# A second level of seven products for gate and up tiles 8 and 9 in a float32 recurrent block

## The chip, the cores and the metric

The kernel runs on one core of a Trainium2 chip. The metric is the time of one execution on the device in microseconds (us). The kernel before takes 2179.63 us as the median of three runs (2178.49 to 2179.87). The engines are named as the profile names them: PE is the matrix engine (PEld its weight loads), DVE the vector engine, ACT the scalar engine, POOL the GpSimd engine, and SP the engine that issues most DMAs.

## The reference, cut to what matters

x has shape 8 x 1024 x 512, all values are float32. One part of the block is a recurrent attention (`s`), the other a gated network (`g`) whose three weight matrices are looked up from 16 values:

```python
xn = layernorm(x)
gate = xn @ lut[gate_idx].T        # 1376 x 512 indices
up = xn @ lut[up_idx].T            # 1376 x 512 indices
h = silu(gate) * up
g = silu(h @ lut[down_idx].T)
out = x + s * g                    # s: three decayed causal scores over xn, gated, times Wo
```

The change touches only gate and up: for each of 8 batches, 1024 tokens by 1376 outputs, twice.

## The kernel before, in words

**Phase 1** (the first 606 us) normalizes and transposes x, runs the attention chunk by chunk, and in between builds the weight matrices from their indices: `ffn_weights` is a generator of which a few steps are taken after each piece of attention (`build_some`), and what is left is run off after the last chunk. Most of these steps are one or two DVE instructions; sums of weights are on POOL. The results go to DRAM.

**Phase 2** goes through the 8 batches: first gate and up, then the down projection (`down_pair`, four pairs of token chunks), which also adds x and writes the output.

Gate and up together are treated as one 2 x 2 block product and computed with seven products in place of eight (the scheme of Strassen and Winograd): the rows are gate and up of one output tile of 128, the columns are the halves of 512 tokens, and the contraction is two halves of 256. The 1376 outputs make eleven tiles: ten of 128 and a last of 96.

- Tiles 0 to 7 form two groups of four (`quads`, NQ = 2). There each of the seven products is itself computed with seven products of half its width, so one `Node` (line 713) stands for one outer product: 7 inner products, each for two pairs of tiles (`a` in 0, 1, side by side in one PSUM bank), each a float32 matmul of 256 columns. The profile counts two PE instructions for one float32 matmul, so that a node is 28 instructions at line 730. The inner products of the next node are mixed between those of the present one (`first`, `fifth` at lines 827 to 835), so that PE always has a product to do while DVE and ACT work on the banks. The output of a node goes through four steps `empty(t, n)`, one for each bank, which differ by outer product (lines 809 to 815).
- Tiles 8, 9 and 10 are done by `single` (line 671) with the outer seven products alone: 14 matmuls of 512 columns, 28 instructions at line 684. In batch 0, tiles 8 and 9 come before the groups of four, since the sums of x needed by the groups are not yet there; in batches 1 to 7 they come after them.

Four big temporaries hold partial results: `p1` and `u2` in pool `tmp`, `u3` and `e5` in pool `tmp2`. The singles take turns in `p1` and `u2`; `down_pair` uses all four. The weights of a node or a single come by a DMA on SP into `ring`, which has three buffers. The second level overwrites one block of x (`xs[:, :, 1, :]`) by a difference; the singles need the block itself, so it is loaded again at the end of the groups (`restore`, line 776, DMAs issued by POOL). `keep_order` at the end fixes the order of PE, DVE, ACT and POOL to the order of the program; SP's order is the planner's.

In phase 1, `gate_up(o)` (line 232) writes the weights of tile o for the singles to `wgu_d[o]`, and for every second tile below 8 also the weights of the second level to `quad_d` (lines 258 to 273): four POOL instructions over 128 x 896, three DMAs and six more steps of the generator.

Of the kernel before, what the change touches and what calls it, by code (L numbers as in the profile page):

```python
# [9 lines left out]
F32 = mybir.dt.float32  # L10
# [27 lines left out]
def recurrent_block(ctx: ExitStack, tc, x, wq, wk, wv, wo, wg, decay_logits, out_scale, lut, gidx, uidx, didx, out):  # L38
# [15 lines left out]

    nc = tc.nc
    B, T, V = x.shape
    D = wq.shape[1]
# [17 lines left out]

    wgu_d = [dram.tile([P, 14, m], F32, name=f"wgud{o}", tag=f"wgud{o}") for o, (_, m) in enumerate(OCH)]

    quad_d = [dram.tile([P, 7, 2, 7 * P], F32, name=f"quadd{q}", tag=f"quadd{q}") for q in range(NQ)]  # L80
    wd_d = [dram.tile([P, 7 * V // 2], F32, name=f"wdd{j}", tag=f"wdd{j}") for j in range(NK)]
    wdt_d = dram.tile([OCH[-1][1], V], F32, name="wdtd", tag="wdtd")
    xs_d = [dram.tile([P, 14, U], F32, name=f"xsd{b}", tag=f"xsd{b}") for b in range(B)]
# [139 lines left out]
    def ffn_weights(build, pool, pair_pool):  # L223
# [8 lines left out]
        def gate_up(o):  # L232
            s, m = OCH[o]
            n = 2 * NV * m
            idx = build.tile([P, NB], I32, name="idx", tag="idx", bufs=2)
            iv = idx[:, :n].rearrange("p (a b) -> p a b", b=m)
            gs, us = (src[:, s : s + m].rearrange("(c p) b -> p c b", p=P) for src in (gidx, uidx))
            nc.sync.dma_start(out=iv[:, 2:6, :], in_=gs)
            nc.sync.dma_start(out=iv[:, 0:2, :], in_=us[:, 0:2, :])
            nc.sync.dma_start(out=iv[:, 6:8, :], in_=us[:, 2:4, :])  # L240
            yield
            wf = pool.tile([P, 2 * NB], F32, name="wgu", tag="wgu", bufs=2)
            yield from look_up(build, wf[:, :n], idx[:, :n], P, n)
            w = wf[:, : 2 * n].rearrange("p (k two m) -> p k two m", two=2, m=m)
            a21, a11, a12, a22, s1, s2, s3, s4 = (w[:, k] for k in range(8))
            nc.gpsimd.tensor_tensor(s1, a21, a22, ALU.add)
            nc.gpsimd.tensor_tensor(s2, s1, a11, ALU.subtract)
            yield
            nc.gpsimd.tensor_tensor(s3, a11, a21, ALU.subtract)
            nc.gpsimd.tensor_tensor(s4, a12, s2, ALU.subtract)  # L250
            wide = wf[:, 2 * m : 2 * n].rearrange("p (a b) -> p a b", b=m)
            defer(3, lambda: nc.sync.dma_start(out=wgu_d[o], in_=wide))
            if o >= 4 * NQ:
                return
            if o % 2 == 0:
# [377 lines left out]
    def phase_2():  # L633
        with (
# [11 lines left out]
            def bank(role, name):  # L646
                return psp.tile([P, U], F32, name=name, tag=role)
# [20 lines left out]
                    nc.gpsimd.tensor_tensor(o, x1, x2, ALU.subtract)  # L668
                    yield

            def single(b, o, xs, h, h_tail, at_last):

                s, m = OCH[o]
                w = ring.tile([P, 14, P], F32, name=f"wr{b}_{o}", tag="wr")
# [1 line left out]
                ho = h[:, o, :] if o < 2 * NK else h_tail  # L676
                ha, hb = ho[:m, :U], ho[:m, U:]
                pa, pb, pe, pc = (bank(r, f"f{r}{b}_{o}")[:m, :] for r in ("s11", "s12", "sE", "s21"))
                t = tmp.tile([P, 4, U], F32, name=f"t{b}_{o}", tag=("u2", "p1")[o % 2])
                u2, u3, e, sg = (t[:m, k, :] for k in range(4))  # L680

                def product(ps, k, start, stop):
# [30 lines left out]
            class Node:  # L713
# [2 lines left out]

                def __init__(self, b, q, k, xs):
                    self.k, self.xs = k, xs  # L720
                    self.w = ring.tile([P, 2, 7, P], F32, name=f"wq{b}_{q}_{k}", tag="wr")
                    nc.sync.dma_start(
                        out=self.w.rearrange("p a t m -> p a (t m)"), in_=quad_d[q][:, W_OF[k], :, :]
                    )
                    self.t = [bank(r, f"{r}{b}_{q}_{k}") for r in ("s11", "s12", "s21", "sE")]
                    self.name = f"e{b}_{q}_{k}"

                def product(self, n, i, start=False):
                    for a in range(2):
                        nc.tensor.matmul(  # L730
                            self.t[n][:, ts(a, H)],
                            lhsT=self.w[:, a, (0, 1, 6, 2, 3, 4, 5)[i - 1], :],
                            rhs=self.xs[:, X_OF[self.k], D_OF[i], :],
                            start=start and a == 0,
                            stop=False,
                            skip_group_check=True,
                        )
# [17 lines left out]
                def seventh(self):  # L755
                    self.product(2, 7)
                    nc.vector.tensor_tensor(self.t[3], self.t[2], self.e, ALU.add)  # L757

            def quads(b, xs, h):


                def two(ap):
                    return ap.rearrange("p (a t) -> p a t", a=2)

                def steps(q):
                    p1, u2, u3, e5 = (
                        pool.tile([P, 4, U], F32, name=f"{k}{b}_{q}", tag=k)
                        for k, pool in (("p1", tmp), ("u2", tmp), ("u3", tmp2), ("e5", tmp2))
                    )

                    def of_h(half, n):
                        r, c = divmod(n, 2)
                        t = half * U + c * H
                        return h[:, 4 * q + r : 4 * q + r + 3 : 2, t : t + H]

                    def restore(*ks):

                        for k in ks if q == NQ - 1 else ():
                            nc.gpsimd.dma_start(out=xs[:, X_OF[k], 1, :], in_=xs_d[b][:, 2 * X_OF[k], H:])

                    def add(o, other):
                        return lambda t, n: nc.vector.tensor_tensor(o[:, n], t[n], other[:, n], ALU.add)  # L782
# [16 lines left out]

                    def after_7():  # L800
                        on_gpsimd(u2, e5)
                        restore(1, 6, 5, 7)

                    def after_4():
                        restore(2, 3, 4)
                        multiply(1, e5)
                        multiply(0, u3)

                    yield 1, lambda t, n: nc.scalar.copy(p1[:, n], t[n]), None
                    yield 6, add(u2, p1), None  # L810
                    yield 5, lambda t, n: nc.scalar.copy(e5[:, n], t[n]), None
                    yield 7, add(u3, u2), after_7
                    yield 2, add(p1, p1), lambda: on_gpsimd(e5, u3)
                    yield 3, node_3, None
                    yield 4, node_4, after_4

                todo = [(q, step) for q in range(NQ) for step in steps(q)]
                node = Node(b, 0, todo[0][1][0], xs)
                node.first()
                node.fifth()  # L820
                node.fifth_copy()
                for n, (q, (k, empty, after)) in enumerate(todo):
                    following = Node(b, todo[n + 1][0], todo[n + 1][1][0], xs) if n + 1 < len(todo) else None
                    node.sixth()
                    node.product(0, 2)
                    empty(node.t, 0)
                    if following:
                        following.first()
                    node.seventh()
                    empty(node.t, 3)  # L830
                    node.product(1, 3)
                    empty(node.t, 1)
                    if following:
                        following.fifth()
                        following.fifth_copy()
                    node.product(2, 4)
                    empty(node.t, 2)
                    if after:
                        after()
                    node = following  # L840

            def some(weights, n):
                for _ in range(n):
# [88 lines left out]
            for b in range(B):  # L932
# [11 lines left out]
                first_sums = sums_of_x(xs, True) if b == 0 else iter(())  # L944
                some(first_sums, 3)
                for o in early:
                    single(b, o, xs, h, h_tail, at_last)
                some(first_sums, 7)
                if b == 0:
                    nc.sync.dma_start(out=wd_tail[: OCH[-1][1], :], in_=wdt_d)  # L950
                    for src, dst in zip(wd_d, wd_sb):
                        nc.sync.dma_start(out=dst, in_=src)
                quads(b, xs, h)
                for o in range(4 * NQ, NO):
                    if o not in early:
                        single(b, o, xs, h, h_tail, at_last)
                t = got[-1]
                more = iter(())
                for c in range(NC // 2):
# [53 lines left out]
```

## Time and profile before

| What | Value |
|---|---|
| median of the runs | 2179.63 us |
| the profiled execution, its own time | 2179.92 us |
| its span, first to last instruction | 2178.1 us |
| granted PE clock | 1.000 |
| DVE, ACT, POOL busy | 51%, 38%, 42% |
| start of phase 2 on PE (line 684, batch 0) | 610.0 us |
| instructions at line 684 (singles), line 730 (nodes) | 672, 3136 |
| DMA, mean | 140 GB/s |

A row of the profile's groups reads: line, engine, operation, output <- inputs, shape, count, then busy time and the mean duration of one, then the idle time of the engine just before. PE's instructions overlap, so that the mean duration of one (380 ns for 256 columns) is longer than the distance to the next; a stretch of PE is therefore measured from start to start. A wait stands under the line that waited, with the engine and line that it waited for.

### The profile page before, as it was taken

The page shows a single profiled execution, that of the slowest core. Times are in us where ns is not written, and L with a number is a line of the kernel's source. Part 1 is how long each engine was busy: PE and PEld are TensorE (multiplying, and loading weights), DVE is VectorE, ACT ScalarE, POOL GpSimd, SP SyncE. Part 2 cuts the span into 40 slices and gives each one's busy share as a digit, 9 for nine tenths or more (in the row PEclk, how much of TensorE's full clock was granted, in tenths as well). Part 3 has the DMA queues.
Part 4 walks back from the last instruction along what each step waited for, and adds up shares of the span by engine and source line. Part 5 has one row for each costly group of instructions (what it writes and reads, how often), then busy time and mean ns, then how long its engine had stood idle before and what let it go on. Part 6 is the DMA issues. An engine that isn't in the chain of part 4 may idle for free.

```text
span 2178.1 us, 25266 instructions
## 1 busy us (share of the span) xinstructions
PE 2167.8 (100%) x9234; PEld 1599.0 (73%) x9234; DVE 1117.3 (51%) x1589; ACT 830.1 (38%) x1795; POOL 918.3 (42%) x800
## 2 busy tenths in 40 slices
PE   9999999999999999999999999999999999999998
PEld 6666666666768778588857867885787688578866
DVE  6888678688635435443533543353344335433533
ACT  3666666666334224313411431242144124313411
POOL 3554544253245453434525442452535154434512
PEclk9999999999999999999999999999999999999999
DMA  7777654554374334234522433443244234334501
GB/s 187 195 192 174 211 191 146 143 142 151 134 291 157 131 113 153 93 131 136 175 93 101 151 114 116 140 162 123 83 147 139 106 118 153 95 127 148 165 25 54
DMA packets 137153, 305.29 MB, mean 140 GB/s; under 512 B 50147, under 2 KB 71910, under 8 KB 136006
## 3 DMA queue, kind: packets, MB, share of 16 engines
q1 hardware_dynamic: 127190, 279.03, 40.2%
q0 software_dynamic: 7728, 23.86, 3.0%
q8 instruction: 73, 1.20, 0.2%
q10 hardware_dynamic: 2112, 0.79, 0.1%
q14 instruction: 50, 0.41, 0.1%
HBM read 225.72 MB, written 77.93 MB: 139 GB/s over the span
## 4 chain that ended last, share of the span: by engine, by line
PE 96%; DMA 1%; POOL 1%; issue 1%; DVE 0%; ACT 0%; SPq 0%; POOLq 0%
PE s L730 27%; PE ds L874 22%; PE fs L684 9%; PE pq L407 9%; PE pv L370 7%; PE sE L730 4%; PE fsE L684 4%; PE po L535 4%; PE ds L885 2%; PE ps L896 2%; PE psc L513 2%; PE pu L521 2%; PE pt L363 1%; PE pk L504 1%; DMA gTd<-g 1%
## 5 line engine op out<-in xcount | busy, mean ns | idle before, releaser
L730 PE MATMUL s<-xs,wq 128*128 128x256 f32 x2688 | 602.9, 380 | 0.0
L730 PEld LDWEIGHTS s<-xs,wq 128*128 128x128 f32 x2688 | 508.7, 190 | 78.4 <-DVE sE L757 2.7
L874 PE MATMUL ds<-wd,s 128*128 128x256 f32 x1280 | 286.7, 379 | 0.0
L874 PEld LDWEIGHTS ds<-wd,s 128*128 128x128 f32 x1280 | 243.2, 190 | 33.0
L407 PE MATMUL pq<-xnT,wqk_sb 128*128 128x512 f32 x512 | 230.3, 592 | 0.0
L874 PE MATMUL ds<-wd,h 128*128 128x256 f32 x960 | 222.9, 379 | 0.0
L874 PEld LDWEIGHTS ds<-wd,h 128*128 128x128 f32 x960 | 182.3, 190 | 52.5 <-issue 27.0
L684 PE MATMUL fs<-xs,wr 128*128 128x512 f32 (+1 forms) x480 | 215.3, 592 | 0.0
L786 POOL TENSOR_TENSOR u<-u,e 128x512 f32<-128x512 f32 x64 | 79.9, 1271 | 276.0 <-DVE u L782 276.0
L370 PE MATMUL pv<-wvg_sb,xnT 128*128 128x387 f32 x512 | 177.5, 488 | 0.0
L753 DVE TENSOR_TENSOR s<-s,e 128x512 f32<-128x512 f32 x112 | 78.4, 700 | 188.1 <-ACT s L752 188.1
L684 PEld LDWEIGHTS fs<-xs,wr 128*128 128x128 f32 (+1 forms) x480 | 86.9, 181 | 115.5 <-issue 112.7
L407 PEld LDWEIGHTS pq<-xnT,wqk_sb 128*128 128x128 f32 x512 | 92.4, 190 | 92.1 <-issue 91.8
L899 POOL TENSOR_TENSOR gx<-gx 128x512 f32<-128x512 f32 x63 | 80.3, 1275 | 184.6 <-DVE gx L897 141.1
L370 PEld LDWEIGHTS pv<-wvg_sb,xnT 128*128 128x128 f32 x512 | 92.7, 190 | 54.3 <-issue 1.9
L349 POOL TENSOR_SCALAR rstd<-rstd 128x1 f32<-128x1 f32 x56 | 30.7, 548 | 240.7 <-ACT junk L348 240.2
L668 POOL TENSOR_TENSOR xs<-xs 128x1792 f32<-128x1792 f32 (+1 forms) x38 | 127.8, 3382 | 2.9 <-issue 1.9
L757 DVE TENSOR_TENSOR sE<-s,e 128x512 f32<-128x512 f32 x112 | 78.3, 699 | 85.3 <-PE s L730 85.3
L915 ACT ACTIVATE gx<-ds 128x256 f32<-128x256 f32 x32 | 12.3, 384 | 287.3 <-PE ds L885 287.3
L730 PE MATMUL sE<-xs,wq 128*128 128x256 f32 x448 | 115.0, 379 | 0.0
L748 ACT COPY e<-sE 128x512 f32<-128x512 f32 x112 | 65.6, 586 | 123.7 <-PE sE L730 123.7
L907 DVE TENSOR_TENSOR pw<-ds,pw 128x256 f32<-128x256 f32 x32 | 13.6, 425 | 177.0 <-PE ds L874 177.0
(146 smaller groups left out, 3326.3 us busy)
## 6 DMA issues: line engine op xcount, KB each, us to landing
wq<-quadd SPq DMA_DIRECT2D x112, 896.0 KB, 4.5
xs<-xsd SPq DMA_DIRECT2D x8, 3584.0 KB, 12.4
x<-in_x SPq DMA_DIRECT2D x64, 256.0 KB, 5.3
xsd<-ts SPq DMA_DIRECT2D x8, 2048.0 KB, 7.3
gx<-in_x SPq DMA_DIRECT2D x64, 256.0 KB, 2.9
out<-gx POOLq DMA_DIRECT2D x63, 256.0 KB, 2.3
wr<-wgud SPq DMA_DIRECT2D x16, 896.0 KB, 4.6
ga<-gTd SPq DMA_DIRECT2D x16, 768.0 KB, 4.9
```

The costliest lines, as they stand in the source:

```text
L370: nc.tensor.matmul(pv, lhsT=xnT[:, v, ts(c, P)], rhs=wvg_sb[:, v, :], start=(v == 0), stop=(v == NV - 1))
L407: nc.tensor.matmul(pq, lhsT=wqk_sb[:, v, ts(j, D)], rhs=xnT[:, v, ts(hf, U)], start=(v == 0), stop=(v == NV - 1))
L535: nc.tensor.matmul(po, lhsT=lh, rhs=rh, start=(n == 0), stop=(n == len(prods) - 1))
L668: nc.gpsimd.tensor_tensor(o, x1, x2, ALU.subtract)
L684: nc.tensor.matmul(ps, lhsT=w[:, 2 * W_OF[k] + n, :m], rhs=xs[:, X_OF[k], 2 * n : 2 * n + 2, :], start=start and n == 0, stop=stop and n == 1,
L730: nc.tensor.matmul(self.t[n][:, ts(a, H)], lhsT=self.w[:, a, (0, 1, 6, 2, 3, 4, 5)[i - 1], :], rhs=self.xs[:, X_OF[self.k], D_OF[i], :], s ...
L748: nc.scalar.copy(self.e, self.t[3])
L753: nc.vector.tensor_tensor(self.t[1], self.t[1], self.e, ALU.add)
L757: nc.vector.tensor_tensor(self.t[3], self.t[2], self.e, ALU.add)
L786: nc.gpsimd.tensor_tensor(o[:, n], o[:, n], other[:, n], ALU.add)
L874: nc.tensor.matmul(ps, lhsT=lhs[k][:, n, :], rhs=wd_sb[n][:, ts(D_OF[k], H)], start=start and n == 0, stop=stop and n == NK - 1, skip_grou ...
L899: (nc.vector if end else nc.gpsimd).tensor_tensor(g, g, xr, ALU.add)
```

## The change

In batches 1 to 7, tiles 8 and 9 of gate and up get the second level of seven products too. The four inner blocks are now two tiles by two token quarters, so that one outer product gives one inner product per bank half, and a node computes two outer products side by side: 1 and 6, 5 and 7, 2 and 3. The fourth outer product is computed as one, without the second level (`Fourth`: two tiles, two matmuls of 512 columns each), and its two results are added to `u3`. These nodes follow the groups of four in the same mixed loop. Tile 10 stays a single and takes its temporary from `e5`. Batch 0 stays as it was but for that temporary. Phase 1 builds the weights of the second level for tiles 8 and 9 as well. `u3` and `e5` of a group are now taken after its second node, and `restore` is called at other places: in batches 1 to 7 each block comes back after its last pair.

```diff
-    quad_d = [dram.tile([P, 7, 2, 7 * P], F32, name=f"quadd{q}", tag=f"quadd{q}") for q in range(NQ)]
+    quad_d = [
+        dram.tile([P, 7, n, 7 * P], F32, name=f"quadd{q}", tag=f"quadd{q}") for q, n in enumerate([2] * NQ + [1])
+    ]
...
-            if o >= 4 * NQ:
+            if o >= 2 * NK:
                 return
...
-            def single(b, o, xs, h, h_tail, at_last):
+            def single(b, o, xs, h, h_tail, at_last, room):
...
-                t = tmp.tile([P, 4, U], F32, name=f"t{b}_{o}", tag=("u2", "p1")[o % 2])
+                t = room.tile([P, 4, U], F32, name=f"t{b}_{o}", tag="e5" if room is tmp2 else ("u2", "p1")[o % 2])
...
+                    if q < NQ:
+                        nc.sync.dma_start(out=w, in_=quad_d[q][:, W_OF[ks[0]], :, :])
+                    else:
+                        for a, k in enumerate(ks):
+                            nc.sync.dma_start(out=w[:, a, :], in_=quad_d[q][:, W_OF[k], 0, :])
...
-                            rhs=self.xs[:, X_OF[self.k], D_OF[i], :],
+                            rhs=self.xs[:, X_OF[self.ks[a]], D_OF[i], :],
...
+            class Fourth:
...
+                    for r in range(2):
+                        nc.sync.dma_start(
+                            out=self.w[:, ts(r, 2), :], in_=wgu_d[4 * NQ + r][:, ts(W_OF[4], 2), :]
+                        )
+                def product(self, r, role):
+                    ps = bank(role, f"{role}{self.b}_4_{r}")
+                    for n in range(2):
+                        nc.tensor.matmul(
+                            ps,
+                            lhsT=self.w[:, 2 * r + n, :],
+                            rhs=self.xs[:, X_OF[4], ts(n, 2), :],
+                            start=n == 0,
+                            stop=n == 1,
+                            skip_group_check=True,
+                        )
+                    o = self.u3[:, ts(r, 2), :]
+                    return lambda: nc.vector.tensor_tensor(o, ps.rearrange("p (a t) -> p a t", a=2), o, ALU.add)
+                def first(self):
+                    self.product(0, "s11")()
+                def fifth(self):
+                    self.add = self.product(1, "sE")
+                def fifth_copy(self):
+                    self.add()
...
+                def pair_steps():
+                    (p1, u2), (e5, u3) = (
+                        (t[:, :, :H], t[:, :, H:])
+                        for t in (tmp.tile([P, 4, U], F32, name=f"{k}{b}_l", tag=k) for k in ("p1", "u2"))
+                    )
...
+                    def node_16(t, n):
+                        nc.scalar.copy(p1[:, n], t[n][:, :H])
+                        nc.vector.tensor_tensor(u2[:, n], t[n][:, H:], p1[:, n], ALU.add)
+
+                    def node_57(t, n):
+                        nc.scalar.copy(e5[:, n], t[n][:, :H])
+                        nc.vector.tensor_tensor(u3[:, n], t[n][:, H:], u2[:, n], ALU.add)
+                        nc.gpsimd.tensor_tensor(u2[:, n], u2[:, n], e5[:, n], ALU.add)
+
+                    def node_23(t, n):
+                        nc.vector.tensor_tensor(p1[:, n], t[n][:, :H], p1[:, n], ALU.add)
+                        nc.scalar.activation(of_h(0, n), p1[:, n], AF.Silu)
+                        nc.vector.tensor_tensor(of_h(1, n), t[n][:, H:], u2[:, n], ALU.add)
+                        nc.scalar.activation(of_h(1, n), of_h(1, n), AF.Silu)
+
+                    def after_57():
+                        for n in (0, 3, 1, 2):
+                            nc.gpsimd.tensor_tensor(e5[:, n], e5[:, n], u3[:, n], ALU.add)
+                        restore(5, 7)
+
+                    def after_23():
+                        restore(2, 3)
+                        for half, other in ((1, e5), (0, u3)):
+                            for n in (0, 3, 1, 2):
+                                nc.gpsimd.tensor_tensor(of_h(half, n), of_h(half, n), other[:, n], ALU.mult)
+
+                    yield (1, 6), node_16, lambda: restore(1, 6)
+                    yield (5, 7), node_57, after_57
+                    yield (2, 3), node_23, after_23
...
+                    if pair:
+                        for ks, empty, after in pair_steps():
+                            yield Node(b, NQ, ks, xs), empty, after
+                        yield Fourth(b, xs, room[0]), None, None
+                    yield None, None, None
...
-                for o in range(4 * NQ, NO):
-                    if o not in early:
-                        single(b, o, xs, h, h_tail, at_last)
+                single(b, NO - 1, xs, h, h_tail, at_last, tmp2)
```

Here `pair` is `b > 0`, and in the groups of four `restore` is now called with 4 alone after the last node where `pair` holds. The order inside the loop is unchanged: sixth and second product of the node, first of the following one, seventh, third, fifth of the following one, fourth.

More of the change, by code (lines that the diff above doesn't have):

```diff
@@ L713, in phase_2, with __init__ @@
             class Node:
[L719 to L726, printed above, removed]
+                def __init__(self, b, q, ks, xs):
+                    self.ks, self.xs = ks, xs
+                    name = f"{b}_{q}_{ks[0]}"
+                    self.w = ring.tile([P, 2, 7, P], F32, name=f"wq{name}", tag="wr")
+                    w = self.w.rearrange("p a t m -> p a (t m)")
+                    if q < NQ:
[3 more added lines that the diff above has]
+                            nc.sync.dma_start(out=w[:, a, :], in_=quad_d[q][:, W_OF[k], 0, :])
+                    self.t = [bank(r, f"{r}{name}") for r in ("s11", "s12", "s21", "sE")]
+                    self.name = f"e{name}"
                 def product(self, n, i, start=False):
@@ L757, in seventh, with __init__, restore @@
                     nc.vector.tensor_tensor(self.t[3], self.t[2], self.e, ALU.add)
+            class Fourth:
+                def __init__(self, b, xs, u3):
+                    self.b, self.xs, self.u3 = b, xs, u3
+                    self.w = ring.tile([P, 14, P], F32, name=f"w4{b}", tag="wr")
+                    for r in range(2):
[21 more added lines that the diff above has]
+                    self.add()
             def quads(b, xs, h):
+                pair = b > 0
+                def restore(*ks):
+                    for k in ks:
+                        nc.gpsimd.dma_start(out=xs[:, X_OF[k], 1, :], in_=xs_d[b][:, 2 * X_OF[k], H:])
                 def two(ap):
@@ L765, in steps, with room_for @@
                 def steps(q):
[L766 to L769, printed above, removed]
+                    def room_for(k, pool):
+                        return pool.tile([P, 4, U], F32, name=f"{k}{b}_{q}", tag=k)
+                    p1, u2 = room_for("p1", tmp), room_for("u2", tmp)
                     def of_h(half, n):
@@ L774, in of_h @@
                         return h[:, 4 * q + r : 4 * q + r + 3 : 2, t : t + H]
-                    def restore(*ks):
-                        for k in ks if q == NQ - 1 else ():
-                            nc.gpsimd.dma_start(out=xs[:, X_OF[k], 1, :], in_=xs_d[b][:, 2 * X_OF[k], H:])
                     def add(o, other):
@@ L801, in after_7 @@
                         on_gpsimd(u2, e5)
-                        restore(1, 6, 5, 7)
+                        if q == NQ - 1 and not pair:
+                            restore(1, 6, 5, 7)
                     def after_4():
-                        restore(2, 3, 4)
+                        if q == NQ - 1:
+                            restore(*((4,) if pair else (2, 3, 4)))
                         multiply(1, e5)
                         multiply(0, u3)
-                    yield 1, lambda t, n: nc.scalar.copy(p1[:, n], t[n]), None
@@ L810, in steps @@
[L810 to L818, printed above, removed]
+                    yield (1, 1), lambda t, n: nc.scalar.copy(p1[:, n], t[n]), None
@@ new lines, in steps, with of_h @@
+                    yield (6, 6), add(u2, p1), None
+                    u3, e5 = room_for("u3", tmp2), room_for("e5", tmp2)
+                    yield (5, 5), lambda t, n: nc.scalar.copy(e5[:, n], t[n]), None
+                    yield (7, 7), add(u3, u2), after_7
+                    yield (2, 2), add(p1, p1), lambda: on_gpsimd(e5, u3)
+                    yield (3, 3), node_3, None
+                    yield (4, 4), node_4, after_4
+                def pair_steps():
[3 more added lines that the diff above has]
+                    )
+                    room[0] = u3
+                    def of_h(half, n):
+                        r, c = divmod(n, 2)
+                        t = half * U + c * H
+                        return h[:, 4 * NQ + r, t : t + H]
+                    def node_16(t, n):
[22 more added lines that the diff above has]
+                    yield (2, 3), node_23, after_23
@@ new lines, in quads, with every @@
+                room = [None]
+                def every():
+                    for q in range(NQ):
+                        for ks, empty, after in steps(q):
+                            yield Node(b, q, ks, xs), empty, after
+                    if pair:
[3 more added lines that the diff above has]
+                    yield None, None, None
@@ L819, in quads @@
+                todo = every()
+                node, empty, after = next(todo)
                 node.first()
@@ L821, in quads @@
                 node.fifth_copy()
-                for n, (q, (k, empty, after)) in enumerate(todo):
-                    following = Node(b, todo[n + 1][0], todo[n + 1][1][0], xs) if n + 1 < len(todo) else None
+                while empty:
+                    following, empty_next, after_next = next(todo)
                     node.sixth()
@@ L839, in quads @@
                         after()
-                    node = following
+                    node, empty, after = following, empty_next, after_next
             def some(weights, n):
@@ L946, in phase_2 @@
                 for o in early:
-                    single(b, o, xs, h, h_tail, at_last)
+                    single(b, o, xs, h, h_tail, at_last, tmp)
                 some(first_sums, 7)
@@ L953, in phase_2 @@
                 quads(b, xs, h)
-                for o in range(4 * NQ, NO):
-                    if o not in early:
-                        single(b, o, xs, h, h_tail, at_last)
+                single(b, NO - 1, xs, h, h_tail, at_last, tmp2)
                 t = got[-1]
```

## The prediction

> **What bounds the kernel now.** I read the page first, then the waits of PE, then the order of time around the end of gate and up in one batch.
>
> ```profile
> PE 2167.8 (100%) x9234; PEld 1599.0 (73%) x9234; DVE 1117.3 (51%) x1589; ACT 830.1 (38%) x1795; POOL 918.3 (42%) x800
> ...
> PE 96%; DMA 1%; POOL 1%; issue 1%; DVE 0%; ACT 0%; SPq 0%; POOLq 0%
> ```
>
> PE is busy all the time, and the chain that ended last is PE for 96%. The waits of PE are four:
>
> ```profile
> PE po L535 <- DVE pr L515: 1.5, 1, 1.5
> PE warm L311 <- POOL nhalf L125: 1.4, 1, 1.4
> PE po L535 <- POOL qb L492: 1.3, 1, 1.3
> PE zs L931 <- ACT bl L536: 0.4, 1, 0.4
> ```
>
> So less PE work is less time, as long as the cover on other engines holds. PE in batch 1, last two nodes of the groups, first single, start of tile 10:
>
> ```profile
> 878.85 5.34 PE L730 MATMUL s<-xs,wq 128*128 128x256 f32 x24
> 884.02 1.03 PE L730 MATMUL sE<-xs,wq 128*128 128x256 f32 x4
> 884.89 5.67 PE L730 MATMUL s<-xs,wq 128*128 128x256 f32 x24
> 890.39 3.60 PE L684 MATMUL fs<-xs,wr 128*128 128x512 f32 x8
> ...
> 914.42 3.60 PE L684 MATMUL fs<-xs,wr 128*96 128x512 f32 x8
> ```
>
> From the 4 fifth products at 877.98 to those at 884.02 is one node: 6.04 us for 28 instructions, 0.2157 each. From 890.39 to 914.42 are tiles 8 and 9: 24.03 us for 56 instructions of 512 columns, 0.429 each. The last node's row is 5.67 long where its like is 5.34: 0.33 lost, because no following node is mixed in; the waits of the weight loads have this as DVE line 757, 2.7 us in 8 cases. Batches 3 and 7 show the same lengths.
>
> **PE, per batch 1 to 7.** Removed: 24.03. Added: three nodes, 84 instructions x 0.2157 = 18.12, and the fourth product, 8 instructions x 0.429 = 3.43; sum 21.55. Difference 2.48. The 0.33 also goes, since the last node of the groups now has a follower, and node (2,3) has the fourth product mixed in; tile 10 follows it as it followed tile 9. **2.81 x 7 = 19.7 us.**
>
> [...]
>
> **What must keep up, with the clock of batch 1.** A product of 4 short instructions is 0.863. The last node of the groups starts at 885.75 and with its follower mixed in ends at 891.79; node (1,6) ends at 897.83, (5,7) at 903.87; (2,3) holds 5 products and 3.43 of the fourth, so it ends at 911.62.
>
> DVE and ACT: a node gives DVE two adds of 700 ns and at most eight 256-wide ones of 425 (line 907), node (2,3) two adds for the fourth as well: 1.4 + 3.4 + 1.4 = 6.2 of 7.75 us. ACT has at most eight SiLUs of 417 (line 917) and a copy: 3.9. Both fit.
>
> POOL is the one to watch, since it is late at that place:
>
> ```profile
> 878.75 4.96 POOL L786 TENSOR_TENSOR e<-e,u 128x512 f32<-128x512 f32 x4
> 883.67 1.11 POOL L779 DMA_DIRECT2D xs<-xsd  x2
> 888.92 0.55 POOL L779 DMA_DIRECT2D xs<-xsd  x1 [4.15 <-PE s L730]
> 889.49 4.95 POOL L790 TENSOR_TENSOR h<-h,e 128x512 f32<-128x512 f32 x4
> 894.40 4.94 POOL L790 TENSOR_TENSOR h<-h,u 128x512 f32<-128x512 f32 x4
> ```
>
> After the change the first multiply waits for the seventh product, which comes 0.5 later, so the eight multiplies run from 890.0 to 899.9. Behind them in the queue: two restores (0.55 each) to 901.0, four adds u2 += e5 of node (5,7), four adds e5 += u3, four restores, eight multiplies. What waits for them: DVE's add of the fourth product to u3 (it may not overwrite what e5 += u3 still reads), DVE's use of u2 in (2,3), the sums of `at_last`, the restored blocks of tile 10.
>
> What does a 256-wide add on POOL cost? Two rows are near:
>
> ```profile
> L911 POOL TENSOR_TENSOR pw<-pw 128x256 f32<-128x256 f32 x32 | 34.5, 1079 | 134.4 <-DVE pw L910 134.4
> ...
> L668 POOL TENSOR_TENSOR xs<-xs 128x256 f32<-128x256 f32 x7 | 4.8, 727 | 0.0
> ```
>
> Seven in a row take 4.83, so 0.69 from start to start; line 911 is 0.71 at best and 1.16 in the median. [...] So I take 0.69; 1.16 is the upper end. With 0.69 the u2 adds follow DVE and end at 905.1 (the last bank is emptied at 904.4), the third add e5 += u3 ends at 907.2; the fourth product's first half is done on PE at 907.3. No wait. With 1.16 DVE waits to 909.1, and its add for line 757 is done at 910.5; PE needs that bank at 910.76: still no stall. With 1.27, the price of 512 columns, PE would lose 0.6 per batch. **I take 0; ends 0 and 4.6 us in all.**
>
> The rest hides: restores of 2 and 3 are issued by 910 and land 2.4 later (median of such restores), tile 10 reads block 2 at 916.8; the last multiply ends near 916.5, `at_last` reads at 920.9; both covers are over 4 us. Weights: a ring buffer comes free 7.7 us before its node starts, and 896 KB land in 4.5, as in the groups now. In the program as built the second pair of x loads for `down_pair` now stands before the load of the next x on SP and waits for that last multiply; the x load waits for tile 10's end (923.6) anyway. Batch 0: tile 10's first copy now waits for `e5`, about 2 us; its next reader of that bank, the second product, is three products later. Nothing.
>
> **Phase 1.** Added: four POOL instructions over 128 x 896 (2.22 to 2.44 each by lines 264 to 270, 9.3 in all), three DMAs of 3.1 MB, six generator steps. The four sets that exist cost PE at most the one wait of 1.3 for POOL's qb; a fifth costs a quarter of that, 0.3 (ends: -1.5, a shifted wait may vanish, to 3). The six steps push the rest of the build back, and five or six of its DVE instructions, 6.5 us, now come after the last attention chunk: DVE is free at about 612 in place of 605, and the first single needs it at 613.75. POOL's last weight sums end near 615 in place of 607.7; its sums of x (12.1 us) then at 627, needed by the first node at 634.9. The late DMA of the last down weights has `fbl` behind it on SP, which waits for its landing (5 us), and behind that the weights of the first node: issued near 622 in place of 616.9, with 11.9 to landing, that is 634, when PE wants them. I take 0.2, ends 0 and 3.
>
> **Sum.** Span 2178.1 - 19.7 + 0.3 + 0.2 = 2158.9. Around the span lie 1.8 us (2179.92 - 2178.1): 2160.7. The profiled run is 0.3 above the median of the runs: **2160.4 us**, 0.9% less.
>
> **Rivals.**
> 1. POOL is late and DVE blocks PE for part of the gain. For it: POOL's backlog of 10 us at that place. Against: the slack above. At 0.6 to 1.2 us per batch the time is 2165 to 2169.
> 2. A single delay in phase 1 or at its seam: the weights of the first node land late, or the shifted build makes the attention wait. For it: the DMA share is 1.0 from 612 to 632. Up to 6 us: 2162 to 2167.
> 3. Slower: the same chain through POOL, with a price above all rows. From 901.0 seven adds of length d must end before DVE's add of the fourth, then 1.39 us of DVE, then PE at 910.76: PE loses 7d - 8.4. The gain of 2.81 is used up at d = 1.60 us; at d = 2.0 the loss is 5.6, so 2.8 x 7 = 20 us more than before: 2199. For it: DVE is 80% busy in that node. Against: no 256-wide row has a median over 1.16.
> 4. The change does not do what it says: nodes of tiles 8 and 9 are held apart by waits on the shared temporaries, and the gain is lost evenly: 2179. Against: in the program as built, PE's short matmuls there wait only for weights and for bank copies.
>
> **How the numbers follow.** Chances: forecast (2157 to 2162.5) 0.64, rival 1 0.19, rival 2 0.09, rival 3 0.05, rival 4 0.03. The range 2157 to 2168 takes in the forecast, most of rivals 1 and 2, and the unknown costs (0 to 4.6, -1.5 to 3, 0 to 3). Faster by over 0.2% (what a measurement can tell from no change, 4.4 us): 0.92; within 0.2%: 0.03; slower: 0.05.
>
> **What would show it.** In the new profile: 28 PE instructions of a pair node in 6.04 us; node (2,3) in 7.75; from the end of the groups to tile 10 21.5 us; PE waits for DVE line 757 in one batch, not eight; the 256-wide POOL adds near 0.7, and the DVE add of the fourth waiting for PE, not POOL. Phase 2 starts at 610 within 2 us. It is wrong if PE waits for DVE in node (2,3), if POOL's short adds take over 1.2, or if phase 1 is longer by more than 3 us.

## The result and the profile after

The changed kernel takes 2158.78 us (median of four runs, 2158.67 to 2159.59) against 2179.15 us for four runs of the kernel before taken with them; the ratio is 0.9907, 95% interval 0.989 to 0.9924. The profiled execution has a span of 2156.9 us, 21.2 less than before. The forecast was 2160.4.

The page and the waits of PE after the change (a wait: total us, times, longest):

```profile
PE 2147.4 (100%) x9486; PEld 1647.1 (76%) x9486; DVE 1158.4 (54%) x1701; ACT 863.9 (40%) x1900; POOL 979.8 (45%) x902
...
PE 98%; POOL 1%; issue 0%; ACT 0%; DVE 0%; DMA 0%; POOLq 0%
```

```profile
PE po L538 <- POOL qb L495: 1.4, 1, 1.4
PE warm L314 <- POOL nhalf L128: 1.4, 1, 1.4
PE pt L366 <- DVE x L358: 0.7, 2, 0.4
PE zs L1033 <- ACT bl L539: 0.4, 1, 0.4
```

PE has 252 instructions more, is busy 20 us less, and is still the only bound: every one of these waits lies in phase 1 or between it and phase 2. Line numbers are now higher (730 has become 737, 757 has become 764, 684 has become 687). No wait in the new nodes is on the list.

The order of time on PE in batch 1, from the last mixed products of node (5,7) to tile 10:

```profile
895.26 5.34 PE L737 MATMUL s<-xs,wq 128*128 128x256 f32 x24
900.44 1.03 PE L737 MATMUL sE<-xs,wq 128*128 128x256 f32 x4
901.31 2.75 PE L737 MATMUL s<-xs,wq 128*128 128x256 f32 x12
903.90 1.88 PE L780 MATMUL s<-xs,w 128*128 128x512 f32 x4
905.61 1.89 PE L737 MATMUL s<-xs,wq 128*128 128x256 f32 x8
907.34 1.88 PE L780 MATMUL sE<-xs,w 128*128 128x512 f32 x4
909.06 1.03 PE L737 MATMUL s<-xs,wq 128*128 128x256 f32 x4
909.92 3.60 PE L687 MATMUL fs<-xs,wr 128*96 128x512 f32 x8
```

Node (2,3) starts after the first four instructions of the row at 901.31, that is at 902.17, and ends at 909.92: 7.75 us. The rows at 903.90 and 907.34 are the fourth product, mixed in; each start follows the one before it at the price of its columns (0.43 us each at 512 columns, 0.216 at 256). The stretch from the start of the groups' last node to tile 10 is 25.88 us (884.04 to 909.92) where it was 28.67 (885.75 to 914.42): 2.79 per batch.

The span splits at the start of phase 2, the first instruction of the first single on PE: 610.05 before, 608.34 after. **Phase 2 took 1568.05 us and takes 1548.56: 19.5 less.** The other 1.7 lie in phase 1.

### The profile page after: what moved, and what is told of

The parts are those of the page before. It is cut to its first block, busy times and chain, and to the rows that moved or that the text cites. A ratio compares the mean times of both kernels' runs of the same rounds, so it can differ in the third digit from the quotient of the medians.

```text
span 2156.9 us, 26203 instructions
## 1 busy us (share of the span) xinstructions
PE 2147.4 (100%) x9486; PEld 1647.1 (76%) x9486; DVE 1158.4 (54%) x1701; ACT 863.9 (40%) x1900; POOL 979.8 (45%) x902
## 4 chain that ended last, share of the span: by engine, by line
PE 98%; POOL 1%; issue 0%; ACT 0%; DVE 0%; DMA 0%; POOLq 0%
PE s L737 32%; PE ds L976 22%; PE pq L410 10%; PE pv L373 8%; PE sE L737 5%; PE fs L687 4%; PE po L538 4%; PE ds L987 2%; PE ps L998 2%; PE psc L516 2%; PE pu L524 2%; PE fsE L687 2%; PE pt L366 1%; PE pk L507 1%; PE sE L780 1%; PE s L780 1%
## 5 line engine op out<-in xcount | busy, mean ns | idle before, releaser
L737 PE MATMUL s<-xs,wq 128*128 128x256 f32 x3192 | 715.1, 379 | 0.0
L737 PEld LDWEIGHTS s<-xs,wq 128*128 128x128 f32 x3192 | 605.6, 190 | 94.1 <-issue 7.0
L760 DVE TENSOR_TENSOR s<-s,e 128x512 f32<-128x512 f32 x133 | 93.0, 700 | 202.2 <-ACT s L759 202.2
L764 DVE TENSOR_TENSOR sE<-s,e 128x512 f32<-128x512 f32 x133 | 93.0, 699 | 102.6 <-PE s L737 102.6
L737 PE MATMUL sE<-xs,wq 128*128 128x256 f32 x532 | 136.5, 379 | 0.0
L755 ACT COPY e<-sE 128x512 f32<-128x512 f32 x133 | 77.8, 585 | 136.1 <-PE sE L737 136.1
L1017 ACT ACTIVATE gx<-ds 128x256 f32<-128x256 f32 x32 | 12.3, 383 | 285.9 <-PE ds L987 285.9
L759 ACT COPY s<-s 128x512 f32<-128x512 f32 x133 | 75.8, 570 | 96.6 <-PE s L737 96.6
L748 ACT COPY s<-s 128x512 f32<-128x512 f32 x133 | 75.8, 570 | 95.8 <-PE s L737 92.1
L737 PEld LDWEIGHTS sE<-xs,wq 128*128 128x128 f32 x532 | 101.1, 190 | 13.7
```

Source lines behind the costliest of these rows:

```text
L737: nc.tensor.matmul(self.t[n][:, ts(a, H)], lhsT=self.w[:, a, (0, 1, 6, 2, 3, 4, 5)[i - 1], :], rhs=self.xs[:, X_OF[self.ks[a]], D_OF[i], : ...
L755: nc.scalar.copy(self.e, self.t[3])
L760: nc.vector.tensor_tensor(self.t[1], self.t[1], self.e, ALU.add)
```

## The experiments

The runs of the kernel before taken beside the experiments have medians of 2179.6 to 2180.5. For each kernel the time, the ratio to the kernel before with its interval, and from the profile the start and the length of phase 2:

| Kernel | us | ratio (95%) | phase 2 starts | phase 2 |
|---|---|---|---|---|
| changed kernel | 2158.78 | 0.9907 (0.989 to 0.9924) | 608.34 | 1548.56 |
| changed kernel, again (e9) | 2159.93 | 0.9907 (0.9894 to 0.9921) | 609.46 | 1548.64 |
| build only (e1) | 2179.56 | 1.0002 (0.9993 to 1.001) | 611.44 | 1569.66 |
| no build (e2) | 2160.47 | 0.9908 (0.9894 to 0.9923) | 608.97 | 1548.73 |
| fourth apart (e3) | 2163.16 | 0.9921 (0.9908 to 0.9933) | 608.81 | 1551.49 |
| fourth short (e4) | 2160.12 | 0.9914 (0.9901 to 0.9927) | 609.53 | 1548.77 |
| 4 more on POOL (e5) | 2160.84 | 0.9904 (0.9889 to 0.992) | 611.54 | 1548.86 |
| 8 more on POOL (e6) | 2178.89 | 0.9991 (0.9982 to 1.0001) | 621.83 | 1566.2 |
| 12 more on POOL (e7) | 2215.32 | 1.016 (1.0129 to 1.0192) | 623.58 | 1600.7 |
| all seven (e8) | 2160.55 | 0.99 (0.9884 to 0.9917) | 611.71 | 1547.2 |
| other order of loads (e10) | 2160.24 | 0.9916 (0.9901 to 0.9931) | 608.50 | 1548.6 |
| all seven, other order of loads (e11) | 2156.68 | 0.9893 (0.988 to 0.9907) | 608.90 | 1545.7 |

The start of phase 2 varies by some us between executions, so phase 2 is the sharper measure, except where the loads of the first node come late (e1, e7, e8). The last two columns are each from one profiled execution. That of e6 and that of e7 took 11 us more than the median of their runs, that of e1 3 us more; in e6 and e7 PE waited 9.1 and 6.3 us early in phase 1, so that phase 2 starts late in them.

### The two halves of the change

**Build only (e1)**, on the kernel before:

```diff
-            if o >= 4 * NQ:
+            if o >= 2 * NK:
                 return
```

together with the larger `quad_d`.

> The kernel before with only the building of the second-level weights of tiles 8 and 9 added in phase 1; phase 2 is as before and doesn't use them. Theory (the building hides, and the 1.7 us by which phase 2 started earlier after the change is the landing of one early gate DMA, that has nothing to do with the build): time of before within 2 us, 2177.5 to 2181; phase 2 from its first single to its end as before, 1568.0. Rival (the shifted build makes phase 1 shorter): 2177.4 in every run, with the gain behind 340 us, where the build differs. Rival (the build costs): above 2181.

**No build (e2)**, on the changed kernel:

```diff
-            if o >= 2 * NK:
+            if o >= 4 * NQ:
                 return
...
-                            nc.sync.dma_start(out=w[:, a, :], in_=quad_d[q][:, W_OF[k], 0, :])
+                            nc.sync.dma_start(out=w[:, a, :], in_=quad_d[0][:, W_OF[k], 0, :])
```

> The changed kernel without the building: the pair nodes read the weights of tiles 0 and 1 in place of those of 8 and 9, so tiles 8 and 9 get other values. Theory: the whole gain is in phase 2, so the time is that of the change, 2158 to 2161, and phase 2 takes 1548.6 as in the change. Rival (the build hides only in part): 2155 to 2157.

The build alone changes nothing that can be measured in the time (1.0002); the nodes alone give the whole gain (phase 2 of 1548.73, 0.2 from the changed kernel's). So the gain is PE work in phase 2. The waits of PE in e1 show the seam, though:

```profile
PE po L537 <- DVE pr L517: 1.6, 1, 1.6
PE warm L313 <- POOL nhalf L127: 1.4, 1, 1.4
PE po L537 <- POOL qb L494: 1.4, 1, 1.4
PE s L732 <- DMA wq<-quadd: 1.3, 1, 1.3
```

The fourth row is the first node waiting for its weights. SP's order of time in e1 shows why:

```profile
616.21 0.32 SPq L299 DMA_DIRECT2D wdd<-wgu  x1
...
617.06 0.90 SPq L954 DMA_DIRECT2D wd<-wdd  x1
620.70 0.32 SPq L938 DMA_DIRECT2D fbl<-bld  x1
621.06 1.86 SPq L954 DMA_DIRECT2D wd<-wdd  x4
622.96 22.45 SPq L724 DMA_DIRECT2D wq<-quadd  x4
```

The write of the last down weights is issued at 616.21; `fbl` is issued only at 620.70, and the first node's weights at 622.96, behind the down weights. That is 11.5 us after the start of phase 2; in the kernel before and in e2, which build nothing, it is 6.8 and 6.9. This part of the prediction's seam is shown: the build pushes the load back by 4.7 us.

Whether PE then waits is a second matter. All nine profiles with the build and this order of loads have the same 11.5 us. In six of them (the changed kernel, e3, e4, e5, e6, e9) the weights landed 12.3 to 12.6 us after their issue, and PE's first node followed the single with at most 0.1 us between; in three (e1, e7, e8) they landed after 13.9, and PE waited 1.3. That phase 1 ended late, as the expectations of e9 and e10 have it, doesn't decide it: e5 starts phase 2 at 611.54 and doesn't wait, e1 starts it at 611.44 and does. What differs is what the DMAs move. The same ten microseconds of e5 and then of e1 (columns: stretch, its length, then for PE, PEld, DVE, ACT and POOL the busy time and instructions, then the PE clock, the DMA share, GB/s):

```profile
624.00:634.00 10.00, 10.00 (x25) 4.50 (x24) 1.90 (x3) 2.36 (x4) 5.46 (x3) 1.00 1.02 428
624.00:634.00 10.00, 10.00 (x25) 4.45 (x24) 1.85 (x4) 2.36 (x4) 5.37 (x3) 1.00 1.02 389
```

The DMA engines are busy throughout in both (share 1.02); in the six profiles without the wait they move 426 to 429 GB/s behind that issue, in the three with it 389. Why one execution moves less than another stays open.

### Mixing the fourth product in

**Fourth apart (e3)**:

```diff
-                        yield Fourth(b, xs, room[0]), None, None
...
                     node, empty, after = following, empty_next, after_next
+                if pair:
+                    node = Fourth(b, xs, room[0])
+                    node.first()
+                    node.fifth()
+                    node.fifth_copy()
```

> The fourth product comes after the last pair node and isn't mixed into it. Theory: node (2,3) then has no follower and loses 0.33 us, as the last node of the groups did before: 7 x 0.33 = 2.3 us more, 2161.0; PE waits for the bank of the sE add of that node in seven batches more. Rival (mixing the fourth in costs by DVE's wait for GpSimd, so that setting it apart saves): 2158.7 or less.

Phase 2 is 2.9 longer, expected were 2.3. PE in batch 1:

```profile
901.98 5.73 PE L737 MATMUL s<-xs,wq 128*128 128x256 f32 x24
907.54 1.88 PE L780 MATMUL s<-xs,w 128*128 128x512 f32 x4
```

The 24 instructions with the unmixed end of node (2,3) take 5.73 in place of 5.34: 0.39 x 7 = 2.7. It is the same wait for the bank of the sE add that the kernel before had in every batch: the weight loads wait for that add (DVE line 764) eight times in e3 and once in the changed kernel. The time of 2163.16 is 2.2 above the 2161.0 that was expected; phase 2 accounts for 0.6 of that. So the mixing is worth what the prediction put on it, a little more, and the rival (mixing costs) falls.

### A short matmul against a long one

**Fourth short (e4)**: each matmul of the fourth product is split in two of 256 columns.

```diff
-                        nc.tensor.matmul(
-                            ps,
+                        for c in range(2):
+                            nc.tensor.matmul(
+                                ps[:, ts(c, H)],
...
-                            rhs=self.xs[:, X_OF[4], ts(n, 2), :],
+                                rhs=self.xs[:, X_OF[4], 2 * n + c, :],
```

> The fourth product in 256 columns in place of 512: 16 instructions in place of 8 per batch, the same columns. Theory (a short matmul costs half of a long one to a nanosecond): 16 x 0.2157 = 3.45 in place of 3.43, no change, 2158.7. [...]

Phase 2 is 0.2 longer with 56 more matmul instructions; so is that of e2, which has no more of them than the changed kernel (1548.77 and 1548.73 against 1548.56). A weight load and a 256-column float32 matmul cost here half of a 512-column one, as in the rows before the change (0.2157 and 0.429 us).

### How late GpSimd may be

**4, 8 and 12 more on POOL (e5, e6, e7)**, with k of 4, 8, 12:

```diff
-                    yield (1, 6), node_16, lambda: restore(1, 6)
+                    def after_16():
+                        restore(1, 6)
+                        for n in range(k):
+                            nc.gpsimd.tensor_tensor(idle[:, n % 2], wo_sb[:, :H], wo_sb[:, H:], ALU.add)
+
+                    yield (1, 6), node_16, after_16
```

> Four additions of 128 x 256 on GpSimd put behind the restores of blocks 1 and 6, into a scratch tile that nobody reads. Theory: from there the seven adds up to the one that DVE's add of the fourth product waits for take 4.83 us and have 8.14 us (until PE needs the sE bank, less 1.39 us of DVE), so 4.8 more adds of 0.69 fit: no change, 2158.7. Rival (there is no slack, GpSimd's delay comes through): 4 x 0.69 x 7 = 19 us more, 2178. Rival (GpSimd is never on the path): no change here and in the two runs with more.

> Eight such additions. Theory: 5.5 + 4.83 = 10.35 of 8.14 us, 2.2 us per batch lost: 15.5 more, 2174; PE waits for DVE in node (2,3) of seven batches. Rival (no slack): 39 us more, 2197. Rival (never on the path): 2158.7.

> Twelve such additions. Theory: 8.3 + 4.83 = 13.1 of 8.14, 5.0 us per batch lost: 35 more, 2193.5, slower than the kernel before. Rival (no slack): 58 us more, 2217. Rival (never on the path): 2158.7.

With four, POOL in batch 1 of e5:

```profile
901.58 1.14 POOL L810 DMA_DIRECT2D xs<-xsd  x2
902.73 2.78 POOL L907 TENSOR_TENSOR idle<-wo_sb 128x256 f32<-128x256 f32 x4
905.48 2.77 POOL L885 TENSOR_TENSOR p_l<-p_l,u_l 128x256 f32<-128x256 f32 x4
908.22 2.76 POOL L895 TENSOR_TENSOR u_l<-u_l 128x256 f32<-128x256 f32 x4
```

Four adds take 2.75 us from start to start, 0.69 each. DVE's add of the fourth product starts only at 910.34 in that run, after waiting 1.88 for POOL, and PE doesn't notice: 1548.86. With eight and with twelve, PE does; the one row of each run's waits:

```profile
PE s L737 <- DVE sE L764: 14.0, 7, 2.0
```

```profile
PE s L737 <- DVE sE L764: 33.0, 7, 4.7
```

Seven waits, one in each batch with pair nodes, on the bank named in advance. The times, 2178.89 and 2215.32, are longer than the 2174 and 2193.5 that were expected. With eight (the first row), node (2,3) and what surrounds it take 2.25 longer in batch 1 (start of the last mixed products to the down projection, 913.96 to 937.71, against 900.44 to 921.94); expected were 2.2. Eight adds are 5.5 us, so 3.3 us or 4.7 adds were free, where 4.8 were worked out. Of the 17.6 us of e6's longer phase 2, 15.9 come so. The other 1.7 lie in the last batch, behind a wait of the same length. PE in batch 1 and in the last batch, and the stretch with the clock (columns as above):

```profile
924.73 1.13 PE L737 MATMUL s<-xs,wq 128*128 128x256 f32 x4 [1.99 <-DVE sE L764]
925.70 3.60 PE L687 MATMUL fs<-xs,wr 128*96 128x512 f32 x8
...
2093.29 1.13 PE L737 MATMUL s<-xs,wq 128*128 128x256 f32 x4 [2.00 <-DVE sE L764]
2094.26 5.29 PE L687 MATMUL fs<-xs,wr 128*96 128x512 f32 x8
```

```profile
2096.00:2098.00 2.00, 2.00 (x3) 0.57 (x2) 0.00 (x0) 0.83 (x3) 2.00 (x4) 0.50 0.46 109
```

The eight instructions of tile 10 take 5.29 us there in place of 3.60, at a granted clock of 0.50; in batch 1 the clock stays at 1.00, and in the six batches before the last the waits account for all that is lost. The time of e6 is 0.9991 of before, the gain is gone.

With twelve the wait is 4.7, and the next instruction starts 4.9 later than it would without it, where 5.0 were worked out; but phase 2 is 52 longer and not 35. PE and the granted clock in batch 1:

```profile
924.15 1.88 PE L780 MATMUL sE<-xs,w 128*128 128x512 f32 x4
930.74 2.07 PE L737 MATMUL s<-xs,wq 128*128 128x256 f32 x4 [4.71 <-DVE sE L764]
932.61 5.34 PE L687 MATMUL fs<-xs,wr 128*96 128x512 f32 x8
937.78 1.88 PE L687 MATMUL fsE<-xs,wr 128*96 128x512 f32 x4
```

```profile
910.00:925.00 15.00, 15.00 (x65) 12.08 (x64) 5.87 (x12) 5.96 (x14) 14.98 (x20) 1.00 0.35 107
925.00:931.00 6.00, 1.29 (x4) 0.45 (x3) 2.00 (x4) 0.42 (x1) 6.00 (x10) 0.86 0.00 0
931.00:936.00 5.00, 5.00 (x8) 2.33 (x9) 2.49 (x7) 2.16 (x6) 4.98 (x9) 0.50 0.56 166
936.00:941.00 5.00, 5.00 (x13) 2.00 (x12) 0.69 (x1) 1.75 (x3) 1.70 (x3) 0.99 0.41 148
```

The twelve instructions after the wait take 7.04 us from start to start (930.74 to 937.78) in place of the 4.29 that the changed kernel takes for the same twelve (909.06 to 913.35). After the 4.7 us wait the clock is 0.50 (931 to 936 us); that is 2.75 more in this batch. PE is slower behind all seven waits, by 2.75 to 2.9 us in batches 1, 3, 5 and 7 and by 1.7 in batches 2, 4 and 6. In sum phase 2 has 34 us of waits, 16.5 of slower instructions behind them and 1.6 at its first node.

### A version that takes less

**All seven (e8)**: the fourth outer product becomes a node of its own with one inner product per bank, half a bank wide, and the first two products of tile 10 are mixed into it, since `single` can now be run in steps.

```diff
-                        yield Fourth(b, xs, room[0]), None, None
+                        yield Tail(tail), None, None
...
+                    yield (4,), node_fourth, after_fourth
...
-                    for a in range(2):
+                    for a in range(len(self.ks)):
```

> The fourth outer product gets the second level too, as a node of one product with half-wide banks, and the first two products of tile 10 are mixed into it. Theory: 14 instructions x 0.2157 = 3.02 in place of 3.43 us, 0.41 x 7 = 2.9 us less: 2155.9. Rival (with two-instruction products in node (2,3), which is then 5.2 us long for 4.8 us of DVE, PE waits for DVE): 2159 or more.

The time missed the forecast by 4.6 us, and the profile says where: phase 2 started at 611.71, and its first node waited 1.3 for its weights. Phase 2 itself is 1547.2, or 1545.9 without that wait, 2.7 below the changed kernel. The rival (DVE holds PE up in the shorter node) is not seen: DVE has no row in PE's waits of phase 2. Three more kernels, measured side by side on one chip, take the seam out of it: the changed kernel again (e9), the changed kernel with the loads in another order (e10), and all seven with that order (e11).

```diff
-                    nc.sync.dma_start(out=wd_tail[: OCH[-1][1], :], in_=wdt_d)
-                    for src, dst in zip(wd_d, wd_sb):
-                        nc.sync.dma_start(out=dst, in_=src)
-                quads(b, xs, h)
+                loads = first_loads if b == 0 else None
+                quads(b, xs, h, loads)
```

(`first_loads` issues the same DMAs and that of `fbl`, and is called in `quads` once the first two nodes are set up.)

> The changed kernel once more, on the same chip as the two that follow. Theory: phase 2 takes 1548.6 us in every run (1549.9 where the weights of the first node land 1.3 late), and what varies is phase 1, which ends between 608 and 612. Rival (phase 1 is shortened by the change): phase 2 starts at 608.3 again.

> The changed kernel with the loads of the down weights and of batch 0's attention rows issued behind the weights of the first two nodes. Theory: the wait of 1.3 us of the first node for its weights, seen where phase 1 ended late, can't come up: phase 2 takes 1548.6 in every run, the time is up to 1.3 below e9 and never above it. Rival (the down weights then hold up the third node's weights): phase 2 is longer than 1549.

> The fourth outer product with the second level and mixed with tile 10, as in e8, and the loads ordered as in e10. Theory: 2.7 us below e10 (e8's phase 2 took 1547.2, of which 1.3 was the wait for the first node's weights), phase 2 1545.9. Rival (e8's time of 2160.5 was no accident of phase 1): not below e10.

Phase 2 repeats to 0.1 us (1548.64 and 1548.6). In e9 it starts at 609.46 and not at 608.34 again, so that the rival (the change shortens phase 1) falls. In e10 the first node's weights are issued at 613.63 and land 6.8 us later, 12 us before their node; in e9 they land just before it. So the other order makes room for a late landing. That it saves time is not shown, since e9 had no wait either: e10 was expected at or below e9, and by the median is 0.3 above it, inside its own spread of 2158.86 to 2165.1. e11 is 2156.68 (2156.39 to 2157.97), each of its runs below each run of e9 (2159.40 to 2160.43), and its phase 2 of 1545.7 is 2.9 below e9's. PE in batch 1 of e11:

```profile
901.88 4.91 PE L742 MATMUL s<-xs,wq 128*128 128x256 f32 x22
906.62 0.59 PE L742 MATMUL sE<-xs,wq 128*128 128x256 f32 x2
907.05 1.89 PE L742 MATMUL s<-xs,wq 128*128 128x256 f32 x8
908.78 1.88 PE L688 MATMUL fs<-xs,wr 128*96 128x512 f32 x4
910.50 1.03 PE L742 MATMUL s<-xs,wq 128*128 128x256 f32 x4
911.36 1.88 PE L688 MATMUL fs<-xs,wr 128*96 128x512 f32 x4
```

The node of the fourth product runs through without a gap, its two-instruction products covered by the four-instruction ones of tile 10. This is the fastest of the kernels, 0.9893 of before.

## Why the prediction was right, step by step

- **PE work, 19.7 us: right.** Phase 2 lost 19.5. Short nodes of 6.04, node (2,3) of 7.75, 2.79 per batch where 2.81 were forecast. The working priced a 256-column matmul at half of a 512-column one (0.2157 and 0.429 us), and e4 bears it out.
- **The 0.33 of the unmixed last node: right.** The waits of the weight loads for that bank fell from eight to one, as forecast. Where e3 puts the unmixed end back, it costs 0.39.
- **POOL: price and slack right, one detail wrong.** The short adds cost 0.69 in a row. The prediction had DVE's add of the fourth product wait for PE; it waits for POOL. POOL and DVE in batch 1 after the change:

```profile
899.52 0.74 POOL L885 TENSOR_TENSOR p_l<-p_l,u_l 128x256 f32<-128x256 f32 x1
901.42 1.41 POOL L885 TENSOR_TENSOR p_l<-p_l,u_l 128x256 f32<-128x256 f32 x2 [1.17 <-DVE u_l L884]
903.28 0.72 POOL L885 TENSOR_TENSOR p_l<-p_l,u_l 128x256 f32<-128x256 f32 x1 [0.45 <-DVE u_l L884]
903.96 2.79 POOL L895 TENSOR_TENSOR u_l<-u_l 128x256 f32<-128x256 f32 x4
```

```profile
902.77 0.42 DVE L884 TENSOR_TENSOR u_l<-s,p_l 128x256 f32<-128x256 f32 x1 [1.10 <-ACT u_l L883]
...
906.10 0.69 DVE L789 TENSOR_TENSOR u_l<-s,u_l 128x512 f32<-128x512 f32 x1 [0.85 <-POOL u_l L895]
906.70 0.69 DVE L764 TENSOR_TENSOR sE<-s,e 128x512 f32<-128x512 f32 x1
```

  The last u2 add starts at 903.28. On the clock of this run the working had put it at about 902.7; DVE's add before it waited for ACT's copy of the same bank, which the working left out. So the third e5 add ends after the fourth product's first half, and DVE waits. It costs nothing: the add for line 764 is done at 907.39, and PE asks for that bank at 909.06. e5 shows that 2.8 us more of POOL would have been free as well. That 0.69 would hold there, and not the 1.16 of line 911, was the author's estimate; no 256-wide add or multiply of the pair nodes lasted over 0.75 (lines 885, 895 and 902). Why line 911 takes longer no run shows.
- **Rival 3, slower: its formula holds as far as the wait goes.** PE's loss was put at 7d - 8.4 for a POOL add of d. Eight adds more are as a d of 1.48: 1.95 by the formula (2.2 by the expectation, whose start was read from the new trace), 2.25 measured. Twelve make it slower than before. What the formula lacks is the clock, 0.50 behind e7's wait in batch 1. (At a d of 1.27 the formula gives 0.5 us per batch, 3.5 in all, where the prediction wrote 0.6 and 4.6; only the upper end of a range rests on this.)
- **Phase 1 and the seam, +0.5: too high for this execution.** Phase 2 started 1.7 earlier, not 0.3 later, and that is nearly the whole miss: in spans the forecast was 2158.9 against 2156.9. The build has no part in it: until 45.99 us the two profiles agree on the starts of line 504, and by the next such start, 56.60 before and 54.80 after, the 1.8 have come, while the programs first differ where tile 9's weights are summed, after 300 us. What is gone is the wait of 1.5 at line 535 for DVE, whose add of an early load of gates (`ga`) waits for that load: it starts at 49.39 before and at 47.41 after. The other profiles agree: leaving out e6 and e7 with their longer wait, this add starts at 47.15 to 50.77, and phase 2 starts 560.6 to 561.4 us later in each, with the build or without it. So the 1.7 us are chance, to the good; in e9, the same kernel again, phase 2 starts at 609.46 and the median is 2159.93, 0.5 below the forecast. What moves that load no run shows.
- **The seam's mechanism was right, its size open as stated.** The load is issued 4.7 us later relative to phase 2, where the prediction had about 5; the wait is 0 or 1.3 us, within the 0 to 3 given, and went with the rate of the DMAs (389 GB/s where PE waited, 426 to 429 where it did not).

## What to carry to other kernels

Where PE is at 100% and its waits add up to a few us, count its columns: half the columns cost half the time here (0.2157 and 0.429 us), and the gain came in full because the queue that was late anyway (POOL) still had 3.3 us of slack before the bank that PE needs next. Follow such a queue to that bank and write down the slack in us. Mixing the products of the next unit into the present one is worth keeping up across unlike units: the last node without a follower lost 0.3 to 0.4 us each time, and mixing tile 10 in let even half-size nodes run without a gap. A one-time load at a seam between phases that is queued behind a write (4.5 us from issue to landing here) should be looked at before a gain of 2 us is measured: in e8's profile the late load took 1.3 of its 2.7, and a start of phase 2 at 611.71 the rest.

## What the runs showed of the hardware

Behind each of the seven waits of 4.7 us in e7, PE's next instructions took 1.7 to 2.9 us longer than in the changed kernel; in batch 1 the granted clock was 0.50 from 931 to 936 us. Behind the waits of 2.0 us in e6 they took as long as in the changed kernel in batch 1, at a clock of 1.00, and 1.7 longer in the last batch, at 0.50. What sets the batches apart no run shows. A chain that delayed PE by a few us per batch therefore had a price here that the sum of waits doesn't show: 16.5 us in e7, on top of 34 of waits.

With the DMA engines busy (share 1.02 in e5 and e1), the loads at the start of phase 2 moved at 426 to 429 GB/s in six executions and at 389 in three, and a load of 896 KB landed 1.3 to 1.6 us later in these (13.9 after its issue, against 12.3 to 12.6).
